# Attention weights kept in PSUM beside the scores, and one transpose moved to another pair of banks

## The chip, the cores and the metric

The kernel runs on one core of one Trainium2 chip. The metric is the device time of one execution in microseconds (us). Three runs of the kernel before gave 2523.47, 2530.24 and 2531.26 us; the median is 2530.24.

The engines go by short names: PE is TensorE, DVE is VectorE, ACT is ScalarE, POOL is GpSimd, SP is SyncE. SBUF is the large memory on the core. PSUM is the small one that PE writes its results into; [...] each tile of this kernel's PSUM pool takes one bank.

## The reference

Two graph layers over 2048 nodes with 256 features, for a batch of 8, on one adjacency matrix that is nearly empty (a node has 24 neighbours at most here).

```python
# layer 0: attention, a softmax of its own in each chunk of 256 keys
scores = clip(q @ kc / 8, -10, 10); scores = where(mask == 0, -10, scores)
ctx = softmax(scores, axis=-1) @ vc         # summed over the 8 chunks
x0  = layernorm(x + layernorm(ctx @ Wo.T + bo + x) * gamma + beta)
# layer 1: graph attention, softmax over the neighbours
e = leaky_relu(s_src[i] + s_dst[j]); alpha = softmax(where(adj, e, -inf))
out = layernorm(x0 + elu(alpha @ (x0 @ W)))
```

## The kernel before, in words

**Tiling.** The kernel sorts the nodes by their number of neighbours, 128 to a tile, so that 16 tiles have between 24 and 5 neighbour slots (`CAPS`, the number is S below). It keeps tables in HBM, one row for each node: keys and values for layer 0 (`kv_d`), the projected features for layer 1 (`wh_d`). For a tile it gathers the table rows of every slot: one indirect DMA for each slot, issued by POOL at L489, with 128 row numbers that lie in SBUF. Two slots make a unit (tile `u`); 14 units form a ring in SBUF, so a gather can start when a unit comes free, that is, when PE has summed it.

**Layer 0** takes two batch elements at a time (4 groups, 64 items of one group and one tile). For an item, `scores0` multiplies the gathered keys by the query on DVE (L547, L554), PE turns and sums the products into a PSUM bank of tag `tf` (L566, L576), `softmax0` reads that bank (L590) and makes the weights `al` in SBUF (L607), and `context0` multiplies the gathered values by them. Three quarters of the units are weighted on DVE by `weighted`, a multiplication of two tensors at L501; the last quarter on ACT by `weighted_act` at L507, which takes a weight as a scale operand. PE sums the weighted units in a bank of tag `acc` (L514). `finish0` projects and normalizes (L635, L641, L647); `rows1` turns the result on PE (L307, in the other `tf` bank), ACT copies it out (L658), and PE makes the table rows for layer 1 (L663).

**Layer 1** takes four batch elements at a time (2 halves, 32 items). `softmax1` adds the gathered logits (L680) and makes the weights in place (`z`, called `e`, last step L700); `context1` weights (L501, L507) and sums (L514) two groups; `finish1` normalizes (L738, L741, L470), and POOL scatters rows (L748, L753).

**Order.** `seq` (L764 to L772) lists the items: layer 0 for groups 0 and 1; then layer 0 for groups 2 and 3 with one layer-1 item of the first half after each two; then the 16 layer-1 items of the second half alone. The loop at L811 issues the gathers one item ahead (`fetch(k + 1)`), then scores, the parts of earlier items, the tables of the next group while there are any (`tables`: L336, L372, L376, L385 on PE into the two banks of tag `tk`, ACT copies at L338, L341, L378, L379, L389, POOL adds beta at L351), then softmax and context. The framework plans the order of each engine's instructions when the program is built, by priorities and its own estimate of times, so it may differ from the order of the source.

**PSUM banks.** Before: `tf` 2, `tk` 2, `acc` 2, `pr` 1, `mf` 1, which makes eight.

## Time and profile before

| | |
|---|---|
| median of three runs | 2530.24 us |
| the profiled execution, its own time | 2397.55 us |
| its span | 2395.8 us |
| busy share of the span: PE, DVE, POOL, ACT | 79%, 77%, 63%, 59% |
| gathers (L489, POOL) | 656 of layer 0, 328 of layer 1 |
| weighting on DVE (L501) | 546 instructions, 648.7 us |
| weighting on ACT (L507) | 1808 instructions |
| DVE busy, PE busy, 197 to 1140 us (layer 0 alone) | 723.56, 837.36 of 943 us |
| DVE busy, PE busy, 1140 to 2000 us (both layers) | 701.91, 679.85 of 860 us |
| DVE busy, PE busy, 2000 to 2396 us (layer 1 alone) | 272.46, 240.48 of 396 us |

Times are of one profiled execution, which took less than the unprofiled runs. A row for a group of instructions gives the line in the program, the engine, the operation, what is written and read with shapes, how many there were, the time they kept the engine busy, the mean duration of one in ns, the idle time in front of them and what ended it. A row of the timeline gives the start and the duration in us; a number in brackets is the time in which the engine did nothing before it. The stretches 197, 1140 and 2000 us were chosen from the items: the first gather starts at 196.9 us, the first layer-1 item is used at 1139 us, and the last layer-0 item's weighting ends at 1946.5 us.

### The profile page before, as it was taken

How to read it: one execution, taken by the hardware profiler on the slowest of the kernel's cores; microseconds unless marked ns; L12 is line 12 of the kernel's file. 1: busy time of each engine (PE TensorE's matmuls, PEld its weight loads, DVE VectorE, ACT ScalarE, POOL GpSimd, SP SyncE). 2: the span in 40 equal slices, each digit the busy share in tenths (PEclk: the TensorE clock that was granted, in tenths of full speed). 3: DMA queues.
4: the chain of work that ended last, by engine and by line, in shares of the span. 5: the costliest groups of instructions: out<-in, count | busy, mean ns of one | idle time of the engine just before them, and what ended most of it. 6: DMA issues, size and time to landing. Idle time of an engine off the chain costs nothing. (4 is left out here: it accounts for less than half of the span.)

```text
span 2395.8 us, 38844 instructions
## 1 busy us (share of the span) xinstructions
PE 1900.4 (79%) x11946; PEld 1622.0 (68%) x11946; DVE 1833.5 (77%) x4099; ACT 1409.0 (59%) x5036; POOL 1505.0 (63%) x1230
## 2 busy tenths in 40 slices
PE   7686889889899898999988885888678786664764
PEld 5565677778778787777876774776566675554653
DVE  6864587877588988588988886887788887775775
ACT  4573455546566555655565665664356677665766
POOL 3125455672666676376668856774677685787883
PEclk9897899899999999999998997987878987877887
DMA  7737877795889798598879977896679896786884
GB/s 259 242 137 272 265 270 281 260 346 209 316 287 320 260 334 319 212 388 298 302 258 353 360 281 238 285 321 221 230 274 326 306 319 248 278 310 231 302 296 154
DMA packets 239982, 669.10 MB, mean 279 GB/s; under 512 B 43688, under 2 KB 70059, under 8 KB 237719
## 3 DMA queue, kind: packets, MB, share of 16 engines
q0 software_dynamic: 156800, 505.01, 60.1%
q1 hardware_dynamic: 79248, 151.55, 17.2%
q10 hardware_dynamic: 3718, 9.97, 1.3%
q8 instruction: 98, 1.61, 0.3%
q14 instruction: 118, 0.96, 0.1%
HBM read 612.79 MB, written 126.36 MB: 309 GB/s over the span
## 5 line engine op out<-in xcount | busy, mean ns | idle before, releaser
L489 POOL DMA_INDIRECT u<-kv_d,idx x656 | 810.2, 1235 | 436.4 <-PE acc L514 185.7
L514 PE MATMUL acc<-ident,u 128*128 128x128 f32 x5248 | 713.4, 291 | 157.0 <-DVE u L501 89.0
L514 PEld LDWEIGHTS acc<-ident,u 128*128 128x128 f32 x5248 | 637.5, 151 | 220.7 <-DVE u L501 133.2
L489 POOL DMA_INDIRECT u<-wh_d,idx x328 | 416.5, 1270 | 148.2 <-issue 76.4
L566 PE MATMUL pr<-ident,u 128*128 128x128 f32 (+1 forms) x1984 | 287.0, 295 | 78.7 <-DVE u L547 77.2
L501 DVE TENSOR_TENSOR u<-u,al 128x1024 f32<-128x1024 f32 x280 | 334.5, 1234 | 1.5
L566 PEld LDWEIGHTS pr<-ident,u 128*128 128x128 f32 (+1 forms) x1984 | 245.4, 151 | 110.8 <-DVE u L547 104.6
L547 DVE TENSOR_TENSOR u<-u,qx 128x1024 f32<-128x1024 f32 (+1 forms) x248 | 302.0, 1218 | 18.3 <-DMA u<-kv_d,idx 15.1
L501 DVE TENSOR_TENSOR u<-u,z 128x1024 f32<-128x1024 f32 x266 | 314.4, 1212 | 0.6
L507 ACT ACTIVATE u<-u,z 128x64 f32<-128x64 f32 x1008 | 262.0, 337 | 25.0 <-DVE z L700 17.1
L507 ACT ACTIVATE u<-u,al 128x64 f32<-128x64 f32 x800 | 209.1, 342 | 23.2 <-DVE al L607 22.3
L663 PE MATMUL mf<-wa,x1T 128*128 128x264 f32 x512 | 167.6, 455 | 23.1 <-ACT x1T L658 14.8
L351 POOL TENSOR_TENSOR xt<-xt,beta_r 128x1024 f32<-128x1024 f32 x32 | 77.1, 2410 | 143.1 <-PE tk L336 126.3
L385 PE MATMUL tk<-wq,xT 128*128 128x256 f32 x512 | 145.2, 397 | 24.4 <-ACT kvs L379 24.4
L451 ACT ACTIVATE nm<-sums 128x2 f32<-128x2 f32 (+1 forms) x160 | 32.4, 202 | 221.3 <-DVE sums L641 122.6
L372 PE MATMUL tk<-wkv,xT 128*128 128x256 f32 x512 | 151.7, 410 | 12.9 <-ACT xC L341 12.6
L635 PE MATMUL mf<-wo,cT 128*128 128x256 f32 x512 | 148.4, 415 | 6.3 <-ACT whs L666 5.3
L376 PE MATMUL tk<-wkv,xC 128*128 128x256 f32 x512 | 144.5, 399 | 0.0
L663 PEld LDWEIGHTS mf<-wa,x1T 128*128 128x128 f32 x512 | 101.7, 218 | 59.7 <-ACT x1T L658 23.6
L455 ACT ACTIVATE sq<-o,nm 128x256 bf16<-128x256 f32 x256 | 129.7, 507 | 5.3
L554 DVE TENSOR_TENSOR u<-u,qx 128x1024 f32<-128x1024 f32 (+1 forms) x96 | 116.0, 1214 | 16.6 <-DMA qx<-qx_d,node 7.1
L590 DVE TENSOR_SCALAR sc<-tf 128x64 f32<-128x64 f32 (+5 forms) x64 | 14.0, 218 | 138.2 <-PE tf L576 138.2
(168 smaller groups left out, 3254.0 us busy)
## 6 DMA issues: line engine op xcount, KB each, us to landing
kv_d<-kvs SPq DMA_DIRECT2D x48, 512.0 KB, 6.0
wh_d<-whs SPq DMA_DIRECT2D x64, 260.0 KB, 5.8
xt<-in_x_dram SPq DMA_DIRECT2D x64, 256.0 KB, 4.8
qx_d<-xt SPq DMA_DIRECT2D x32, 512.0 KB, 4.4
qx_d<-qs SPq DMA_DIRECT2D x64, 256.0 KB, 5.8
x_d<-o SPq DMA_DIRECT2D x64, 256.0 KB, 5.2
xr<-x_d SPq DMA_DIRECT2D x32, 512.0 KB, 4.9
u<-kv_d,idx POOLq DMA_INDIRECT x656, 6.5
```

The lines of the kernel that those rows point to most:

```text
L372: nc.tensor.matmul(pm[:, 0:F], xT[:, b * KC + kc, rows], wkv[:, kc, 0:F], start=(kc == 0), stop=False, skip_group_check=True)
L376: nc.tensor.matmul(pm[:, F:], xC[:, b * KC + kc, rows], wkv[:, kc, F:], start=False, stop=(kc == KC - 1), skip_group_check=True)
L385: nc.tensor.matmul(qb, xT[:, b * KC + kc, rows], wq[:, kc, :], start=(b == 0 and kc == 0), stop=False, skip_group_check=True)
L455: nc.scalar.activation(sq, src[:, k, :], AF.Square, bias=nm[:, k:k + 1], accum_out=m2[:, k:k + 1])
L489: nc.gpsimd.indirect_dma_start(out=u[:, k, 0:width], out_offset=None, in_=table, in_offset=bass.IndirectOffsetOnAxis(ap=idx[:, t, s0 + k:s ...
L501: nc.vector.tensor_tensor(pv, pv, av, op=ALU.mult)
L507: nc.scalar.activation(pe, pe, AF.Copy, scale=al[:, e, s0 + k:s0 + k + 1])
L514: nc.tensor.matmul(acc[:, c, :], part[:, k, c * P:(c + 1) * P], ident, is_transpose=True, start=first and k == 0 and c == 0, stop=last and ...
L547: nc.vector.tensor_tensor(prod.rearrange("p k j (s w) -> p k j s w", w=W8), u[:, :, 0:GF].rearrange("p s (k j w) -> p k j s w", k=UNIT, w=W8),
L566: nc.tensor.matmul(pr[0:n * W8, k, :], prod[:, j // (NJ // UNIT), j % (NJ // UNIT), :], ident, is_transpose=True, start=(j == 0), stop=(j ...
L635: nc.tensor.matmul(po[:, b, :], cT[:, b * KC + kc, :], wo[:, kc, :], start=(b == 0 and kc == 0), stop=False, skip_group_check=True)
L663: nc.tensor.matmul(pw[:, 0:F + 2 * H], xT[:, b * KC + kc, :], wa[:, kc, :], start=(kc == 0), stop=(kc == KC - 1))
```

## The change

The weights of both layers go to PSUM. A new tag `sc` with two banks takes the place of `tf`. In layer 0 a bank holds an item's scores in its first 192 columns and, once these are read, its weights from column 192 on; in layer 1 `softmax1` takes a bank for its weights. `weighted` (L501) then reads the values from SBUF and the weights from PSUM. `weighted_act` still reads them from SBUF, so the last quarter's weights are made a second time there, by one more DVE multiplication for an item that has such units. A bank is held until the item's last weighting on DVE. The transpose in `rows1` uses the tag `tk`, which until now only the tables used. The number of banks stays eight.

```diff
@@ scores0
-        ps_sc = bank("tf")[:, 0:GH * S].rearrange("p (s e) -> p s e", e=GH)
+        scb = bank("sc")
+        ps_sc = scb[:, 0:GH * S].rearrange("p (s e) -> p s e", e=GH)
@@ softmax0
-        nc.vector.tensor_tensor(al, al, ev, op=ALU.mult)
-        st0[g, t] = al
+        w = scb[:, GH * TOP:GH * TOP + n].rearrange("p (e s) -> p e s", s=S)
+        nc.vector.tensor_tensor(w, al, ev, op=ALU.mult)
+
+        first = len(got0[g, t][1]) - len(got0[g, t][1]) // 4
+        if UNIT * first < S:
+            nc.vector.tensor_tensor(al[:, :, UNIT * first:], al[:, :, UNIT * first:], ev[:, :, UNIT * first:], op=ALU.mult)
+        st0[g, t] = w, al
@@ context0
-                weighted(u[:, :, GF:2 * GF], al, s0, n)
+                weighted(u[:, :, GF:2 * GF], w, s0, n)
@@ rows1
-        pt = transposed(o.rearrange("p b f -> p (b f)"), "tf", 2)
+        pt = transposed(o.rearrange("p b f -> p (b f)"), "tk", 2)
@@ softmax1
-        nc.vector.tensor_tensor(e, e, r.unsqueeze(2).to_broadcast([P, 2 * GH, S]), op=ALU.mult)
-        st1[p, t] = e
+        w = bank("sc")[:, 0:2 * GH * S].rearrange("p (e s) -> p e s", s=S)
+        nc.vector.tensor_tensor(w, e, r.unsqueeze(2).to_broadcast([P, 2 * GH, S]), op=ALU.mult)
+        first = len(units) - (len(units) + 2) // 4
+        if UNIT * first < S:
+            nc.vector.tensor_tensor(e[:, :, UNIT * first:], e[:, :, UNIT * first:],
+                                    r.unsqueeze(2).to_broadcast([P, 2 * GH, S - UNIT * first]), op=ALU.mult)
+        st1[p, t] = w, e
@@ context1
-                    weighted(part, e[:, k * GH:(k + 1) * GH], s0, n)
+                    weighted(part, w[:, k * GH:(k + 1) * GH], s0, n)
```

## The prediction

> **What bounds the kernel now.** I read the page first. No engine is full over the span (PE 79%, DVE 77%), so the mean says little, and I went by stretches. In layer 0 alone (197 to 1140 us) PE is busy 837 of 943 us; in layer 1 alone (from 2000 us) it is 240 of 396. The second stretch is where the change acts. The table of stretches, POOL's instructions alone (busy us, count):

> ```profile
> 2000.00:2396.00 396.00, 284.58 (x230) 0.80 0.73 263
> 1140.00:2000.00 860.00, 596.37 (x462) 0.87 0.82 289
> 197.00:1140.00 943.00, 572.52 (x460) 0.94 0.83 292
> ```

> POOL's share looks mild, but the timeline adds 0.30 us of issue before each instruction. From 2100 to 2300 us POOL has 127 instructions, busy 161.3 us; with 127 x 0.30 that is 199.4 of 200 us. So POOL sets the pace there, and what lengthens its gathers counts. POOL's timeline, then DVE's:

> ```profile
> 2224.74 1.00 POOL L489 DMA_INDIRECT u<-wh_d,idx  x1 [0.30 <-issue]
> 2226.04 2.03 POOL L489 DMA_INDIRECT u<-wh_d,idx  x1 [0.30 <-DVE u L501]
> 2228.38 1.97 POOL L489 DMA_INDIRECT u<-wh_d,idx  x1 [0.31 <-PE acc L514]
> 2230.65 1.96 POOL L489 DMA_INDIRECT u<-wh_d,idx  x1 [0.30 <-DVE u L501]
> ...
> 2239.23 0.99 POOL L489 DMA_INDIRECT u<-wh_d,idx  x1 [0.30 <-issue]
> 2240.53 1.00 POOL L489 DMA_INDIRECT u<-wh_d,idx  x1 [0.30 <-PE acc L514]
> ```

> ```profile
> 2225.99 8.02 DVE L501 TENSOR_TENSOR u<-u,z 128x1024 f32<-128x1024 f32 x7
> 2233.94 0.61 DVE L680 TENSOR_TENSOR z<-u,sd 128x32 f32<-128x32 f32 x5
> ...
> 2242.50 0.22 DVE L680 TENSOR_TENSOR z<-u,sd 128x32 f32<-128x32 f32 x1 [4.53 <-DMA u<-wh_d,idx]
> 2245.92 0.21 DVE L680 TENSOR_TENSOR z<-u,sd 128x32 f32<-128x32 f32 x1 [3.20 <-DMA u<-wh_d,idx]
> ```

> While L501 runs, a gather takes about 2 us; after it, 1.00. And DVE then waits for gathers. I took the start of every indirect DMA against DVE's timeline: 312 started with DVE idle (mean 0.995 us), 56 during the reduction L556 (1.000), 238 during L501 (1.680), 162 during L547 (1.431), 53 during L554 (1.505). L501, L547 and L554 read two tensors from SBUF. L738 and L641 read one from PSUM and one from SBUF: 22 starts, 1.000, and 31 starts, 0.995.

> [...] at 512 columns, with and without a PSUM input:

> ```profile
> L738 DVE SCALAR_TENSOR_TENSOR xr<-mf,xr 128x512 f32<-128x512 f32 x64 | 43.8, 684 | 21.5 <-ACT hT L737 9.9 <-DMA xr<-x_d 7.5 <-SPq L868 4.1
> L547 DVE TENSOR_TENSOR u<-u,qx 128x512 f32<-128x512 f32 x20 | 13.6, 679 | 0.1
> ```

> From start to start both take 602 ns at the median. [...]

> **The change, part by part.**

> *Removed: the hold on POOL.* 238 starts x (1.680 - 0.995) = 163 us of POOL time, in three stretches. A part of it is worth something only where DVE waits for a gather.
> - 2000 to 2396 us: POOL's 230 instructions take 284.6 us; at 1.00 each it would be 230, so 54.6 us are excess, of which 52.9 began under L501. DVE's waits for layer-1 gathers (L680) are 63.6 us here. The ceiling is 53. Next in line is DVE: from 2100 to 2300 us it is busy 143.6 us, and POOL without the hold would need 199.4 - 34.5 = 165 us, where DVE would stand at 87%. With its round trips to ACT and PE this won't all be reached, so I take 38 us. Scatters (L753) share POOL's queue and come earlier too.
> - 1140 to 2000 us: 78 us of excess under L501, but DVE waits for gathers only 16.8 + 6.5 + 6.2 + 2.9 = 32.4 us. Around the tiles of 24 and 13 slots gathers land as they are used; elsewhere 10 us or more before. Taking for each item the smaller of its excess and its wait gives 18 us, and I take 15.
> - 197 to 1140 us: 31 us of excess, 12.7 us of waits, PE near full: 5 us. Here the gathers of most items land 10 to 40 us before use; that cover hides the rest.

> Gain: 38 + 15 + 5 = 58 us.

> *Unchanged in size: L501 from PSUM.* [...] I take 0, from the two rows above. [...]

> *Added: the second multiplications.* Layer 0: tiles with 7 slots or more have units on ACT, 14 of 16 tiles, 56 items. Layer 1: all 32 items. The nearest row, L607, takes about 0.2 us, and 0.12 us from start to start; 88 x 0.12 = 10.6 us, at most 17.6. It stands between the softmax and the first L501, on the chain from scores to sums, behind it on DVE everything of the item. I take 10 us. Writing the weights to PSUM rather than SBUF has no row; [...] I take nothing.

> *The bank `sc`.* For each layer-0 item I compared the first L576 with the last L501 of the item that would hold the same bank two turns before. The least distance is 14.7 us, mostly 20 to 45. In layer 1 it is DVE behind itself. No wait: nothing. The cover is DVE's own order, since the products that L576 sums come after those weightings on DVE.

> *Moved: `rows1` to `tk`.* No instruction more or less: four PE transposes and one ACT copy of 0.58 us, on the same queues, no DMA. But most of these 64 uses fall beside the tables' 188 uses from 197 to 1430 us, and PE already waits for these banks:

> ```profile
> PE tk L372 <- ACT xC L341: 7.0, 5, 1.8
> PE tk L336 <- ACT kvs L379: 5.7, 1, 5.7
> PE tk L336 <- ACT qs L389: 3.7, 6, 2.3
> PE tk L385 <- ACT kvs L379: 2.9, 1, 2.9
> ```

> That is 19.3 us (the wait list of PE for 197 to 1403 us). Laying the transposes into the sequence of `tk` uses as the trace has them, 39 uses would start before the use two earlier was copied out, late by 82 us in sum. Queued behind such a use on PE are the score turns L566 and L576, for which DVE waits at L590 already (95.7 us from 197 to 1140 us), and L336, for which POOL waits at L351 with gathers behind it. The plan can put other PE work in front, so the bound is 0 to 82 us; I take 20. After 1403 us the tables are done and nothing is lost.

> Sum: -58 + 10 + 20 = -28 us, 2397.6 to 2370 us, against the profiled execution. The runs' median is 1.055 times the profiled time; -28 x 1.055 = -30 us, so 2500 us.

> **The rivals.**
> - *More comes through* (0.12): the whole of 53 and 32 us and 6, less 10: -81 us, some 2445. For it: no POOL gap over 0.31 us from 2100 to 2300. Against: DVE at 87% then.
> - *Hidden anyway* (0.10): layer 1's pace passes to the ring or DVE at once, and half the gain covers the losses: 2525 to 2535. For it: POOL waits 220 us over the whole run for PE to free units.
> - *The `tk` banks* (0.17, slower): the plan leaves the transposes where they are, PE pays 82 us: +82 + 10 - 58 = +34, some 2566. It decides against the change from 48 us of stall on. For it: PE's 89% in layer 0; against: nothing of `rows1` is urgent, so the plan has room.
> - *The hold stays* (0.06): L501 would have SBUF first and PSUM second, and L738 and L641 have it the other way round; if the side matters, only the losses are left: +30, 2562.

> **How the numbers follow.** Forecast 0.55, its own range 2468 to 2522. Differences under 0.3% (7.6 us) can't be told from none. Faster: 0.55 + 0.12 and a little of the hidden case, 0.69; within: 0.08; slower: 0.23. The low end 2448 takes in most of the first rival; the high end 2555 all of the hidden case and the lesser part of the two slow ones.

> **What would show it.** Right: L489's means (1235 and 1270 ns) fall to about 1.10 us for layer 0, where L547 and L554 still hold, and 1.00 for layer 1; L680's wait for DMA falls below 30 us; POOL shows gaps after 2000 us; L501 stays at 1.22 us. Wrong: [...] PE waits on `tk` of 50 us or more before 1403 us, with L590's wait grown; or L489 unchanged.

## The result, and the profile after

The changed kernel takes 2637.14 us (median of four runs, 2620.03 to 2662.57) against 2527.55 us of the kernel before (2523.47 to 2531.26). The ratio is 1.039, with a 95% interval of 1.034 to 1.045: slower, where 2500 us and a gain were forecast. Medians below are of all runs; the ratios leave out single executions that took over 1.5% more than the fastest of their kernel, so the two can differ a little.

One thing has to be known to read any number here: the same kernel comes out at one of two times. The kernel before takes 2385 to 2388 us in some groups of runs and 2527 to 2542 us in others. Its profile (2397.55 us) belongs to the faster condition, while its timed runs above belong to the slower one. The profile after (2642.95 us, span 2641.2 us) is of the slower one. I call the two conditions the first and the second kind. The expectations below say "kind of chip", but whether it is the chip or a state that it was in, no run tells: chip number 15 stood for the first kind in one group and for the second in another. Every ratio is taken against the kernel before in the same group of runs.

The shorter gathers that the prediction counted on are in the trace. Groups of instructions (line, engine, operation, tiles and shapes, count; busy us and mean ns; idle time in front and what ended it), of the kernel before and then of the changed one:

```profile
L489 POOL DMA_INDIRECT u<-kv_d,idx x656 | 810.2, 1235 | 436.4 <-PE acc L514 185.7 <-issue 138.2 <-DMA qx_d<-qs 26.8
L489 POOL DMA_INDIRECT u<-wh_d,idx x328 | 416.5, 1270 | 148.2 <-issue 76.4 <-PE acc L514 34.5 <-ACT sq L455 12.6
L501 DVE TENSOR_TENSOR u<-u,al 128x1024 f32<-128x1024 f32 x276 | 332.0, 1242 | 1.5
L501 DVE TENSOR_TENSOR u<-u,z 128x1024 f32<-128x1024 f32 x264 | 313.1, 1216 | 0.6
```

```profile
L490 POOL DMA_INDIRECT u<-kv_d,idx x656 | 719.6, 1097 | 618.5 <-PE acc L515 354.7 <-issue 177.3 <-DMA kv_d<-kvs 26.1
L502 DVE TENSOR_TENSOR u<-u,sc 128x1024 f32<-128x1024 f32 x540 | 639.1, 1213 | 0.2
L490 POOL DMA_INDIRECT u<-wh_d,idx x328 | 344.9, 1051 | 288.2 <-PE acc L515 152.1 <-issue 88.5 <-remote 16.8
L751 DVE SCALAR_TENSOR_TENSOR xr<-mf,xr 128x512 f32<-128x512 f32 x64 | 44.1, 689 | 82.2 <-ACT hT L750 61.1 <-DMA xr<-x_d 11.9 <-issue 8.9
L549 DVE TENSOR_TENSOR u<-u,qx 128x512 f32<-128x512 f32 x20 | 13.7, 687 | 0.1
```

Gathers fell from 1235 and 1270 ns to 1097 and 1051 ns, and the weighting with a PSUM operand (L502, before L501) costs what it cost. Taken by their starts, 272 indirect DMAs began while L502 ran and took 0.997 us in the mean; the 238 that began under L501 before took 1.680 us. The time went into waits: 354.7 + 152.1 = 506.9 us in which POOL waits for PE to sum a unit, 220.3 before. POOL's stretches, layer 1 alone first (before: 284.58 us busy of 396). A row gives the stretch, its length, POOL's busy time and count, PE's granted clock as a share of full speed, the DMA engines' busy share and GB/s:

```profile
2242.00:2641.00 399.00, 223.68 (x222) 0.76 0.71 254
1140.00:2242.00 1102.00, 579.35 (x524) 0.85 0.74 258
197.00:1140.00 943.00, 465.30 (x406) 0.88 0.72 257
```

POOL is 61 us less busy in layer 1, yet the stretch is as long as before. POOL's timeline, then DVE's, there:

```profile
2365.70 0.97 POOL L766 DMA_INDIRECT out_dram<-xr,nodeb  x1 [0.31 <-issue]
2368.50 1.04 POOL L490 DMA_INDIRECT u<-wh_d,idx  x1 [1.82 <-remote]
```

```profile
2359.37 0.34 DVE L699 TENSOR_TENSOR z<-z,m 128x176 f32<-128x176 f32 x1
2369.30 0.34 DVE L702 TENSOR_TENSOR z<-z,valid 128x176 f32<-128x176 f32 x1 [9.58 <-ACT z L701]
```

POOL's instructions here take about 1.00 us, and DVE stands still for 9.58 us, no longer for a gather but for ACT; and "remote" is new. It stands where a semaphore's update ended the wait, but no instruction in the profile ended near it. DVE's wait leads back to one as well: ahead of L701 in ACT's queue is a copy (L735) that waited 8.30 us for PE's sums and started at 2368.43 us, though the last of these sums (L515) ended at 2360.51 us by the trace. The trace before has no "remote" wait; this one has 326 us of them. From the list of waits after (who waited for what: us in total, times, longest):

```profile
POOL u L490 <- PE acc L515: 506.9, 116, 18.2
...
ACT cT L634 <- remote: 71.4, 14, 19.3
```

PE's waits on the tables' banks, 197 to 1430 us (before, the four rows of L372, L336 and L385 had 19.3 us):

```profile
PE tk L308 <- ACT o L471: 27.1, 16, 3.3
PE tk L386 <- ACT kvs L380: 21.4, 2, 19.2
```

### The profile page after: what moved, and what is told of

Read it like the earlier page. It is cut to its first block, busy times and chain, and to the rows that moved or that the text cites. A ratio compares the mean times of both kernels' runs of the same rounds, so it can differ in the third digit from the quotient of the medians.

```text
span 2641.2 us, 38932 instructions
## 1 busy us (share of the span) xinstructions
PE 1956.3 (74%) x11946; PEld 1683.8 (64%) x11946; DVE 1815.7 (69%) x4187; ACT 1409.2 (53%) x5036; POOL 1320.6 (50%) x1230
## 5 line engine op out<-in xcount | busy, mean ns | idle before, releaser
L490 POOL DMA_INDIRECT u<-kv_d,idx x656 | 719.6, 1097 | 618.5 <-PE acc L515 354.7
L515 PE MATMUL acc<-ident,u 128*128 128x128 f32 x5248 | 735.5, 299 | 135.8 <-DVE u L502 77.0
L515 PEld LDWEIGHTS acc<-ident,u 128*128 128x128 f32 x5248 | 665.1, 156 | 193.7 <-DVE u L502 98.8
L502 DVE TENSOR_TENSOR u<-u,sc 128x1024 f32<-128x1024 f32 (+1 forms) x546 | 642.8, 1207 | 0.2
L490 POOL DMA_INDIRECT u<-wh_d,idx x328 | 344.9, 1051 | 288.2 <-PE acc L515 152.1
L549 DVE TENSOR_TENSOR u<-u,qx 128x1024 f32<-128x1024 f32 (+1 forms) x248 | 291.0, 1173 | 28.9 <-DMA u<-kv_d,idx 21.3
L386 PE MATMUL tk<-wq,xT 128*128 128x256 f32 x512 | 142.4, 403 | 46.8 <-ACT kvs L380 43.3
L593 DVE TENSOR_SCALAR sc<-sc 128x64 f32<-128x64 f32 (+5 forms) x64 | 13.9, 218 | 221.8 <-PE sc L578 160.8
L377 PE MATMUL tk<-wkv,xC 128*128 128x256 f32 x512 | 144.6, 396 | 0.0
L386 PEld LDWEIGHTS tk<-wq,xT 128*128 128x128 f32 x512 | 97.0, 203 | 62.3 <-ACT kvs L380 47.5
L649 DVE CUSTOM_DVE_ANT_0 o<-mf,qx 128x256 f32<-128x256 f32 x128 | 49.2, 419 | 122.6 <-PE mf L314 48.4
L578 PE MATMUL sc<-sel,prT 128*128 128x16 f32 (+1 forms) x496 | 79.4, 284 | 71.2 <-ACT prT L574 53.4
```

What stands on the lines that cost most here:

```text
L377: nc.tensor.matmul(pm[:, F:], xC[:, b * KC + kc, rows], wkv[:, kc, F:], start=False, stop=(kc == KC - 1), skip_group_check=True)
L386: nc.tensor.matmul(qb, xT[:, b * KC + kc, rows], wq[:, kc, :], start=(b == 0 and kc == 0), stop=False, skip_group_check=True)
L490: nc.gpsimd.indirect_dma_start(out=u[:, k, 0:width], out_offset=None, in_=table, in_offset=bass.IndirectOffsetOnAxis(ap=idx[:, t, s0 + k:s ...
L502: nc.vector.tensor_tensor(pv, pv, av, op=ALU.mult)
L515: nc.tensor.matmul(acc[:, c, :], part[:, k, c * P:(c + 1) * P], ident, is_transpose=True, start=first and k == 0 and c == 0, stop=last and ...
L549: nc.vector.tensor_tensor(prod.rearrange("p k j (s w) -> p k j s w", w=W8), u[:, :, 0:GF].rearrange("p s (k j w) -> p k j s w", k=UNIT, w=W8),
```

## The experiments

The kernels were run in groups, each on one chip and with its own runs of the kernel before; a group fell on either kind as it came. I took three parts apart: where the rows' transposes go (tf, tk or mf), and which layer's weights are in PSUM. The expectations of the first four are in absolute times that assume 2530 us for the kernel before; it took 2386 us there, so I read them as differences from it.

### Rows to tk alone; both weights with rows on mf; each layer alone (first kind)

Rows to `tk` alone, the kernel before with

```diff
-        pt = transposed(o.rearrange("p b f -> p (b f)"), "tf", 2)
+        pt = transposed(o.rearrange("p b f -> p (b f)"), "tk", 2)
```

> The kernel before with one edit: the transposes of layer 1's rows go to the tables' banks (tk); weights stay in SBUF, scores stay on tf. Banks theory (the loss of 110 us comes from rows and tables sharing tk): 2600 to 2650 us. Gathers theory (the loss comes from gathers that POOL, no longer held up, issues in bursts ahead of need): 2525 to 2555 us, no burst, gather mean stays near 1235 and 1270 ns. Order theory (the loss comes from the changed order of the instructions on the engines, whatever causes it): anything between 2500 and 2650, not foretold by the weights' place.

Both layers' weights in PSUM, rows on `mf`, the changed kernel with

```diff
-        pt = transposed(o.rearrange("p b f -> p (b f)"), "tk", 2)
+        pt = transposed(o.rearrange("p b f -> p (b f)"), "mf", 1)
```

> The changed kernel with one edit: the transposes of layer 1's rows go to the single bank mf instead of tk; weights of both layers stay in PSUM. Banks theory: the loss goes, 2480 to 2530 us. Gathers theory: the loss stays, 2600 to 2660 us, gather mean near 1097 and 1051 ns. Order theory: not foretold.

Layer 0's weights alone, rows back with the scores:

```diff
-        w = bank("sc")[:, 0:2 * GH * S].rearrange("p (e s) -> p e s", s=S)
-        nc.vector.tensor_tensor(w, e, r.unsqueeze(2).to_broadcast([P, 2 * GH, S]), op=ALU.mult)
...
+        nc.vector.tensor_tensor(e, e, r.unsqueeze(2).to_broadcast([P, 2 * GH, S]), op=ALU.mult)
+        st1[p, t] = e, e
@@ rows1
+        pt = transposed(o.rearrange("p b f -> p (b f)"), "sc", 2)
```

> Only layer 0's weights in PSUM, in the bank of their scores; layer 1's weights in SBUF, and the rows' transposes share the scores' two banks as in the kernel before. Banks theory: 2490 to 2530 us, since tk is not touched. Gathers theory: a loss of 60 to 100 us, 2590 to 2630 us, since layer 0's weightings are the ones that overlap the gathers over most of the span; gather mean near 1100 ns in layer 0, 1250 in layer 1. Order theory: not foretold.

Layer 1's weights alone, rows on `tk`:

```diff
-        w = scb[:, GH * TOP:GH * TOP + n].rearrange("p (e s) -> p e s", s=S)
-        nc.vector.tensor_tensor(w, al, ev, op=ALU.mult)
...
+        nc.vector.tensor_tensor(al, al, ev, op=ALU.mult)
+        st0[g, t] = al, al
```

> Only layer 1's weights in PSUM (turns with the scores), the rows' transposes on tk, layer 0's weights in SBUF. Banks theory: near the changed kernel, 2600 to 2650 us. Gathers theory: a third of the loss, 2540 to 2580 us, lost after 1140 us of the span only. Order theory: not foretold.

Measured, with the kernel before at 2386.30 us: rows on tk 2450.18 us (1.027 [1.023, 1.030]), both weights on mf 2343.72 us (0.981 [0.978, 0.984]), layer 0 alone 2429.29 us (1.017 [1.013, 1.022]), layer 1 alone on tk 2389.03 us (1.001 [0.998, 1.003]).

As differences, the banks theory had both weights on mf right (-43 us), came near with rows on tk (64 us, 70 to 120 expected), and missed with layer 0 alone (43 us more, where a gain or nothing was expected) and layer 1 alone on tk (3 us, 70 to 120 expected). The gathers theory, which forecast losses, missed with both weights on mf, and its 60 to 100 us for layer 0 alone are 43.

So the rows' move costs 64 us by itself, and layer 1's weights bring 61 us on top of it (2450.18 to 2389.03). That speaks against the gathers theory: layer 1's gathers fell from 1269 to 1137 ns between the two, and the time fell with them. The rows' cost is not the one that the prediction priced. The uses of `tk` that wait for a copy-out did not grow in sum (PE L336 on ACT L389 2.2 us, 5.9 before; L372 on L341 7.2, 12.6 before; L385 on L379 26.9, 24.4 before). What grew is PE's wait in front of the transposes for their own operand; PE's waits with rows on tk:

```profile
PE tk L307 <- ACT o L470: 68.0, 34, 6.3
PE tk L385 <- ACT kvs L379: 26.9, 10, 11.8
```

On tf the same wait was 24.0 us. So the transposes reach the head of PE's queue before their rows are ready. That this wait, 44 us longer, makes the 64 us is argued, not shown: in the changed kernel on this kind, run later, it is 53.8 us, and that kernel gains. The 43 us that layer 0's weights cost on banks shared with the rows I can't place, since the list of waits has no row for them. They are not a cost of these weights as such: with the rows on tk, layer 0's weights bring 68 us (2389.03 with layer 1's alone, 2320.76 with both, from two groups).

### The changed kernel again, rows on mf with none, layer 1's or layer 0's weights (second kind)

The edits are those above, in other pairings.

> The changed kernel, unedited, beside the first four experiments' kind of run. Banks theory, with what the first four gave (tk alone +64 us, layer 1's weights on tk -61 us): layer 0's weights take nothing back, so 2370 to 2400 us. Rival (layer 0's weights hold their bank through the weightings, so the next scores wait; they cost 43 us when they shared banks with the rows' transposes): 2425 to 2485 us, and the gap is found at the items whose scores follow a layer 1 item.

> The kernel before with one edit: the rows' transposes on mf; weights in SBUF. If the gain of the both-in-PSUM kernel on mf (-43 us) comes from the weights in PSUM: 2385 to 2410 us. If it comes from taking the rows' transposes out of the scores' banks: 2335 to 2360 us.

> Rows' transposes on mf, layer 1's weights alone in PSUM. If each layer's weights bring about half of the gain: 2360 to 2375 us. If layer 1's bring all of it, as on tk: 2335 to 2350 us. If layer 0's bring all: 2385 to 2400 us.

> Rows' transposes on mf, layer 0's weights alone in PSUM; the two banks sc are then used by scores and layer 0's weights alone. If the loss with the shared banks (+43 us) came from the rows' transposes between two scores: 2350 to 2390 us. If layer 0's weights in PSUM cost by themselves: 2420 to 2440 us.

Here the kernel before took 2541.65 us, 155 more than beside the first four, which none of the four expectations had reckoned with. Changed kernel 2645.87 us (1.032 [1.022, 1.042]); rows on mf alone 2561.61 us (1.010 [1.007, 1.013]); with layer 1's weights 2582.41 us (1.012 [1.004, 1.019]); with layer 0's weights 2609.58 us (1.026 [1.019, 1.034]). Here weights in PSUM bring nothing in layer 1 and cost in layer 0. Either the rows' place or the condition had turned the sign; the same kernels had to be run across.

### The kernels before and after, and both weights on mf, side by side (second kind)

> The kernel before, unedited, for a trace on the same chip as the next two. The first four runs were on a chip where the kernel before takes 2386 us, the next four on one where it takes 2542 us. If the 2542 us come from stretches in which PE, DVE and ACT all stand still although what they wait for is done by the trace (60 us in the profile of the kernel before at 2396 us, 120 us and more in the profiles of the second chip), this trace has 55 to 65 us of such stretches at about 2390 us, or 110 to 130 us of them at about 2540 us.

> The changed kernel, unedited. Theory 1, the loss belongs to the change on either chip: ratio to the kernel before 1.02 to 1.04 here too. Theory 2, the loss is the second chip's alone, and on the first the weights in PSUM pay for the rows' place: ratio 0.98 to 1.01 where the kernel before takes about 2386 us.

> Both layers' weights in PSUM, rows' transposes on mf, again. Theory 1, the place of the rows decides: 0.975 to 0.99 on either chip. Theory 2, the second chip takes the gain: 1.01 to 1.04 where the kernel before takes about 2542 us.

The kernel before took 2542.75 us under the profile, with 111.7 us of stretches of over 1.5 us in which PE, DVE and ACT all stand still, as expected (59.7 us in its profile of the first kind). Changed kernel 2638.06 us (1.041 [1.025, 1.056]). Both weights on mf 2654.47 us (1.049 [1.035, 1.063]), beyond the 1.01 to 1.04 expected at most, and the very kernel that had 0.981 on the first kind. So the condition turns the sign, not the rows' place. This group gives the two traces that can be compared. The list of waits of the kernel before on the second kind, then of the changed kernel:

```profile
POOL u L489 <- PE acc L514: 350.3, 100, 18.7
...
ACT kvs L378 <- remote: 56.2, 9, 19.9
```

```profile
POOL u L490 <- PE acc L515: 508.2, 104, 19.9
...
ACT cT L634 <- remote: 60.0, 13, 10.8
...
ACT kvs L379 <- remote: 53.8, 4, 23.4
DVE o L649 <- remote: 52.6, 3, 26.3
```

One of these waits, of ACT L379, in the changed kernel's timelines, ACT's, PE's and POOL's:

```profile
686.36 0.37 ACT L379 COPY kvs<-tk 128x256 f32<-128x256 f32 x1 [17.97 <-remote]
```

```profile
670.74 0.63 PE L314 MATMUL tk<-ident,biasT 128*128 128x128 f32 x2
689.87 0.47 PE L568 MATMUL pr<-ident,u 128*128 128x128 f32 x1 [18.49 <-DVE u L549]
```

```profile
682.12 1.00 POOL L490 DMA_INDIRECT u<-kv_d,idx  x1 [0.30 <-issue]
683.43 1.00 POOL L490 DMA_INDIRECT u<-kv_d,idx  x1 [0.30 <-issue]
```

ACT's copy at 686.36 us waits for the matmuls of L377, whose last one ends at 658.80 us by the trace. The trace also has the semaphore's updates: PE's five reports after 656 us, from instructions that ended at 656.42, 656.86, 657.94, 658.80 and 671.38 us, came at 663.21, 666.02, 677.94, 686.33 and 687.86 us. Matched in this order they are 6.8 to 27.5 us late, while POOL issues one gather after another. PE's ends are modelled, so the trace can't say whether PE's work or only its reports were late. The stretches around it (length, then busy time and count of PE, its weight loads, DVE, ACT and POOL, PE's granted clock, DMA share, GB/s):

```profile
655.00:670.00 15.00, 7.06 (x30) 5.60 (x29) 2.65 (x8) 2.63 (x10) 11.65 (x12) 0.73 1.00 378
670.00:688.00 18.00, 1.38 (x5) 0.69 (x3) 1.14 (x3) 0.85 (x4) 11.08 (x12) 0.50 0.97 357
```

The granted clock is low here, but by the trace it fell, from full to half, at 661.98 us, after PE had fallen idle at 658.80 us. It then stays at half until 692.70 us, and PE's work is slower for it: four matmuls of 128x256 took 1.03 us at full clock (L377 at 657.77 us) and 1.91 us at half (L386 at 669.03 us).

I counted such waits in every trace: of waits of ACT and DVE of over 1 us that PE's semaphore ended over 1 us after PE's last reporting instruction, the part after that instruction's end. I call it late reports. First kind: 0 us in all kernels. Second kind: kernel before 147.6 us, rows on mf 145.0, layer 1's weights on mf 152.5, layer 0's 204.1, both 223.2, changed kernel 213.3 to 225.2. For the kernel before this is close to what the second kind costs it (2541.0 - 2395.8 = 145 us of span). For the changed kernel it is not: it has 69 us more of them, 216.3 us, and the second kind costs it 2644.5 - 2312.1 = 332 us.

The late reports are densest where POOL issues indirect DMAs, most of them gathers, in an unbroken run (starts less than 1.4 us apart). Share of the time that is late (in pieces of 1 us, such waits of PE and POOL counted too), in the kernel before and the changed one, both of the second kind:

| | outside a run, or its first two | third to sixth gather | seventh and later |
|---|---|---|---|
| kernel before | 56 of 1845 us, 3% | 75 of 525 us, 14% | 71 of 178 us, 40% |
| changed kernel | 82 of 1689 us, 5% | 97 of 715 us, 14% | 111 of 247 us, 45% |

Indirect DMAs that follow another within 1.4 us: 669 before, 840 after. The first kind has as many (656 and 847) and no late reports, so the late reports don't make the runs, and runs alone don't make late reports. Full DMA queues could be the cause as well, since they go with such runs; the next experiments were made to part the two.

### Half the bytes, or broken runs

Half-width tables leave out layer 0's value rows of three groups (shown for the changed kernel; in the kernel before the weights are `al`):

```diff
-    kv_d = [nc.dram_tensor(f"kv_d{g}", [N, 2 * GF + (g == PG)], F32).ap() for g in range(NG)]
+    kv_d = [nc.dram_tensor(f"kv_d{g}", [N, 2 * GF + 1 if g == PG else GF], F32).ap() for g in range(NG)]
@@ context0
-        S = CAPS[t]
+        S, v0 = CAPS[t], GF if g == PG else 0
...
-                weighted(u[:, :, GF:2 * GF], w, s0, n)
+                weighted(u[:, :, v0:v0 + GF], w, s0, n)
...
```

`weighted_act` and `summed` read the same columns.

Spaced gathers:

```diff
             for k in range(n):
+                nc.gpsimd.memset(u[:, k, 0:128], 0.0)
                 nc.gpsimd.indirect_dma_start(
```

> The kernel before with layer 0's tables of three of the four groups at half width (the gathered row is the key half, 2 KB instead of 4 KB), and the weights applied to the key half in place of the value half; it leaves the value rows of these groups out, and does as many instructions as before. Theory A (on the second chip PE's reports come late because the DMA queues are full: 148 us of such waits in the kernel before there, none on the first chip): these waits fall to a third in the stretch up to 600 us and after 1140 us, 50 to 90 us in all, and the time to 2400 to 2460 us on that chip. Theory B (lateness has nothing to do with the DMA load): 130 to 160 us of such waits stay, time above 2480 us. On the first chip: no late reports, 2330 to 2390 us.

> The changed kernel with the same half-width tables. Theory A: late reports fall from 216 us to below 110 us, and the loss against the half-width kernel before shrinks from 105 us to below 45 us. Theory B: they stay near 200 us, and so does the loss near 100 us. On the first chip: no late reports, and the difference of the two half-width kernels lies within 30 us of the difference between the changed kernel and the one before.

> The changed kernel with a memset of 128x128 on POOL ahead of each gather into its own destination, about 200 ns each, 197 us of POOL in all: it gives the gathers back the time that the weights in PSUM took from them (138 ns a gather in layer 0, 219 ns in layer 1). Theory A: late reports fall from 216 us towards 150 us, and the time falls to 2560 to 2620 us on the second chip. Rival (POOL's own time counts, since gathers wait for their buffers and then follow each other): 2650 to 2720 us, late reports as before. On the first chip: slower than the changed kernel by 20 to 80 us.

> The changed kernel unedited, to stand beside the three in the same call. On a chip where the kernel before takes about 2540 us: ratio 1.03 to 1.045, late reports 210 to 230 us. On a chip where it takes about 2386 us: no late reports, and by the sums of the first four runs (rows on tk +64 us, layer 1's weights -61 us, layer 0's weights between -20 and +45 us) a ratio of 0.99 to 1.02.

This group fell on the first kind (kernel before 2387.53 us), with no late reports in any trace, so it settled another question: **the change itself is faster there, 2320.76 us, 0.973 [0.968, 0.977], a gain of 67 us.** It is below the 0.99 that I had expected at best. The half-width kernels took 2468.71 us (before) and 2400.70 us (after): the change brings 68 us at this load too, within the 30 us expected. That half the bytes made the kernel before slower by 81 us I had not expected (2330 to 2390 us). The weighted rows now lie where the products of the scores lay before, which may tie the two together; that is not tested. The spaced kernel took 2443.85 us. Its 984 memsets keep POOL busy for 179 us, and the time grows by 123 us, above the 20 to 80 expected: over the whole kernel, each microsecond of memset cost 0.69 us. Groups of the changed kernel on the first kind, and POOL's stretches (layer 1 alone, both layers, layer 0 alone):

```profile
L490 POOL DMA_INDIRECT u<-kv_d,idx x656 | 730.0, 1113 | 454.6 <-PE acc L515 202.5 <-issue 160.4 <-DMA kv_d<-kvs 26.4
L490 POOL DMA_INDIRECT u<-wh_d,idx x328 | 350.9, 1070 | 183.4 <-issue 78.6 <-PE acc L515 61.1 <-DVE u L502 12.2
```

```profile
1970.00:2312.00 342.00, 224.45 (x222) 0.83 0.81 296
1140.00:1970.00 830.00, 530.24 (x471) 0.91 0.84 303
197.00:1140.00 943.00, 528.12 (x455) 0.93 0.80 290
```

POOL's instructions are as short as on the second kind (224.45 and 223.68 us in layer 1). POOL waits for PE's sums 202.5 + 61.1 = 263.6 us instead of 507, and the layer-1 stretch is 342 us long instead of 399.

The half-width kernel after was run once more and fell on the first kind again, at 2402.21 us (1.007 [1.005, 1.010]), within what was expected there; it parts no theories:

> The changed kernel with the half-width tables again (layer 0's value rows of three groups left out), for a chip of the second kind. In the traces of the second kind the late reports of PE lie where POOL issues gathers without a break: 2 to 7 per cent of the time outside such runs, 36 to 48 per cent from the seventh gather of a run on. Theory P (POOL's unbroken runs of gathers delay PE's reports, whatever they carry): this kernel has as many unbroken runs (622 gathers third or later in a run against 616) and keeps 190 to 260 us of late reports; 2590 to 2650 us, where the first kind gave 2401. Theory A (the load on the DMA queues delays them): this kernel has half the time of full queues (545 us against 1060) and falls below 120 us of late reports; 2480 to 2540 us. On a chip of the first kind: 2390 to 2410 us, no late reports, and nothing told apart.

Then it stood beside the spaced kernel, on the second kind:

> As in the run before this one (the changed kernel, layer 0's value rows of three groups left out): on the second kind of chip theory P (unbroken runs of gathers) keeps 190 to 260 us of late reports and gives 2590 to 2650 us; theory A (full DMA queues) gives less than 120 us of them and 2480 to 2540 us. On the first kind 2385 to 2410 us and nothing told apart.

> The changed kernel with a memset of 128x128 on POOL ahead of each gather, which breaks POOL's runs (159 gathers third or later in an unbroken run, 616 in the changed kernel) at the same bytes; 2444 us on the first kind of chip, 123 us slower than the changed kernel there. On the second kind, theory P: late reports fall from 216 us to between 60 and 120 us, and it takes 2520 to 2580 us, faster than the changed kernel there. Theory A: time of full queues falls only from 1060 to 900 us, so 180 us or more of late reports stay and it takes 2620 to 2720 us. On the first kind: 2435 to 2455 us, nothing told apart.

Half width: 2627.12 us (1.035 [1.026, 1.043]), 200.1 us of late reports. Its gathers moved 392 MB instead of 505, and the time with DMA queues at least 95% busy fell from 840 to 475 us (counted in pieces of 5 us), but the late reports stay near those of the changed kernel, as the runs theory expected. So it is not the bytes in the queues. That it is the number of rows asked for, the same in both kernels, is not tested. Spaced: 2634.45 us (1.037 [1.029, 1.045]), 157.5 us of late reports. Neither theory had this right: the runs theory expected 60 to 120 us and 2520 to 2580 us, the queue theory 180 us or more, though its 2620 to 2720 us hold. With the runs broken there are 59 us less of late reports, about as much as the change had added, and about as many as the kernel before has are left. The 123 us that the memsets cost on the first kind cost nothing here (2634.45 against 2638.06 us of the changed kernel in its own group). So how densely POOL issues gathers seems to set a part of the lateness. This rests on one trace, the memsets (179 us of POOL in this trace too) also delay the gathers, and what sets the rest is open.

All kernels side by side, as ratios to the kernel before:

| rows' transposes | weights in PSUM | first kind | second kind |
|---|---|---|---|
| tk (the change) | both | 0.973 | 1.032 to 1.041 |
| tk | none | 1.027 | |
| tk | layer 1 | 1.001 | |
| mf | both | 0.981 | 1.049 |
| mf | none | | 1.010 |
| mf | layer 1 | | 1.012 |
| mf | layer 0 | | 1.026 |
| tf | layer 0 | 1.017 | |
| tk, spaced gathers | both | 1.024 | 1.037 |

An empty cell was not run. Of the versions tried, the changed kernel is the best on the first kind and the kernel before on the second; none beats both on both.

## Why the prediction was wrong

**The step that failed** is the last line of the sum, "The runs' median is 1.055 times the profiled time; -28 x 1.055 = -30 us". It took the gap of 133 us between the profiled execution and the runs for a factor that stretches everything alike. It was another condition, with waits that the profile in hand did not contain: 147.6 us of PE's late reports in the kernel before, 216.3 us in the changed one. Under it the change costs 104 to 110 us. The late reports are what the traces show in place of the assumed factor; that they make the whole difference is not shown (below). None of the rivals had it; the slow ones ended at 2562 and 2566 us with other mechanisms.

**The sum, against its own profile.** On the first kind the forecast was -28 us and the runs give -67 us: right sign, too small. By the last weighting of an item, in the two traces of that kind, the change brings 10 us up to the end of layer 0 alone (992.8 to 983.0 us), 36 more up to the last item of layer 1's first half (2015.8 to 1970.0 us) and 38 in layer 1's second half (380.0 to 342.1 us): 84 us of span.
- *Removed hold*: the 38 us of layer 1 are what was forecast; as they are net of the other terms and of another stretch (from 2015.8 and not 2000 us), that they agree to the microsecond is luck. The 15 us of the middle stretch were too few; 36 us net is about the whole 32.4 us that DVE waited for gathers there. Of the 31 us in layer 0 alone I took 5; 10 came net of the costs. Waits for a gather look too narrow a measure of what a faster POOL is worth: the spaced kernel lost 0.69 us for each microsecond of memset on POOL, in the mean over all stretches.
- *Moved rows*: 20 us taken, bound 0 to 82; alone they cost 64 us. The size was off, and the mechanism too: what grew is not the wait for a copy-out but PE's wait in front of the transposes. With the weights in PSUM the loss is not seen as such; the two layers' weights together bring 129 us (2450.18 to 2320.76 us).
- *L501 from PSUM*: nothing, as taken (1213 ns, 1216 to 1242 before; at 512 columns, with a PSUM input and without, 689 and 687 ns).
- *Second multiplications*: 174 and about 185 ns each for 88, 15.7 us of busy time, within the 10.6 to 17.6 us assumed.
- *What the hold acts on*: the traces show that an indirect DMA that starts under L501 takes 1.680 us and one that starts under L502 0.997; which step of it takes the longer, no run shows.

On the second kind the same steps are in the trace (the gathers' 1097 and 1051 ns), but each gain is overrun: +68 us by the end of layer 0 alone (1042.1 to 1110.5 us), +27 more by the last item of layer 1's first half, +8 in its second half. A gain of 84 us and 69 us more of late reports would make -15 us; the traces have +103.5, so some 118 us are not accounted for. The count leaves out waits under 1 us and all that queues behind a late report. It also leaves out the clock. From the first kind to the second the granted clock goes from 0.885 to 0.861 in the kernel before and from 0.906 to 0.845 in the changed one, and PE's busy time for the same 11946 matmuls grows by 38 us (1900.4 to 1938.8) and by 122 us (1847.3 to 1968.9). That is 83 us more in the changed kernel; how much of it lengthens the span is not shown. In the case above the clock fell after PE had fallen idle; that it always follows, and is never itself the cause, is not shown. POOL's wait for PE's sums shows that there is more: 263.6 to 508.2 us between the kinds for the changed kernel, 220.3 to 350.3 for the one before. How these add up is not shown.

**The signs.** Right were the gathers' means (1097 ns for 1.10 us, 1051 for 1.00), L688's wait for DMA (14.2 us, forecast below 30; 80.5 before), POOL's gaps in layer 1 and L502's duration. The sign of the `tk` rival came out as well, 27.1 + 21.4 us and 8.3 in smaller rows before 1430 us, with DVE's wait for scores at 160.8 us (138.2 before). It misleads: on the first kind these waits are 42.8 us, and the kernel gains.

## What to carry to other kernels

If the profiled execution and the timed runs differ by more than the runs do among themselves, the profile may be of another condition: get a trace at the time that is to be forecast before a gain is worked out, and don't scale. A faster issuer of DMAs can change the density of issue as well as its own time (here 840 indirect DMAs within 1.4 us of the one before, against 669), so ask what the denser issue meets. A change of three parts should be priced and tried part by part, in each condition in which it will run.

## What the runs showed of the hardware

The kernel before took 2385 to 2388 us in some groups and 2527 to 2542 us in others, and the number that a chip reports does not tell the two apart (15 stood for both). On the first kind the updates of the engines' semaphores follow nearly every end by 0.01 to 0.02 us. On the second, records are missing for every engine: in a trace of the changed kernel there are 1644 updates for PE's 1867 reporting instructions, 2491 for DVE's 3314 and 2387 for ACT's 3055, and no landing times of DMAs. Of the updates that are there, 309 of PE's came over 1 us after the last reporting instruction had ended by the profile, but 13 of ACT's and 2 of DVE's (2 of each on the first kind). So the lateness is PE's; in the example it reaches 27.5 us. Half-width rows left 200.1 us of late reports (213.3 to 225.2 in the changed kernel), broken runs of gathers 157.5 us. What in the chip holds PE or its reports up is open. Every trace of the second kind lacks records and none of the first does, so the recording itself may have a part in the lost time; no run tested that.
